# A Strassen-type scheme for the gates of a gated graph layer: seven f32 block products in place of eight

## The chip, the cores and the metric

The kernel runs on one core of a Trainium2 chip. The metric is device time in microseconds (us) of one execution.

## The reference, cut to what matters

128 graphs of 64 nodes with 256 features pass through four graph layers, each with a residual and a layer norm. Layer 3 is the large one: five rounds of message passing, each with a GRU cell whose gates are products with 256 x 768 weights.

```python
A = (adj != 0).astype(x.dtype)
h = x
for l in range(5):
    m = jnp.einsum('bnd,de->bne', h, weight[l])
    agg = jnp.einsum('bij,bid->bjd', A, m)
    gi = agg @ w_ih.T + b_ih            # r, z and n parts, 256 columns each
    gh = h @ w_hh.T + b_hh
    r = sigmoid(i_r + h_r);  z = sigmoid(i_z + h_z)
    n = tanh(i_n + r * h_n)
    h = (1.0 - z) * n + z * h
```

## The kernel before

It works on 16 chunks of 8 graphs, that is 512 nodes. Layer 0 is done first for all; then two chunks at a time go through layer 3 (`back`), while the middle layers 1 and 2 of the next two chunks (`mid`) run beside them. The weights `weight[l]` and `w_ih` are folded into one matrix `V` per round. Features lie on partitions in two halves `j` (outputs) and `k` (inputs), and nodes along the 512 columns of a bank of PSUM, the memory that takes TensorE's products (other tiles lie in SBUF). One round of one chunk:

```python
for j in range(2):
    pr, pz, pn, pi = (pg.tile([128, NP * 128], F32, tag="pg", name=f"p{s}") for s in ("r", "z", "n", "i"))
    for p, q, last in ((pn, 4 + j, True), (pr, j, False), (pz, 2 + j, False)):
        for k in range(2):
            nc.tensor.matmul(p, WHH[:, k, q * 128 : (q + 1) * 128], hT[:, k, :], start=k == 0, stop=last and k == 1)
    for p, q, first in ((pr, j, False), (pi, 4 + j, True), (pz, 2 + j, False)):
        for k in range(2):
            nc.tensor.matmul(p, V[:, l, k, q * 128 : (q + 1) * 128], agg[:, k, :], start=first and k == 0, stop=k == 1)
    # ... r: sigmoid (ScalarE); r = (pn + bhh) * r; r = pi + r (VectorE); n: tanh; z: sigmoid (ScalarE)
    nc.vector.tensor_sub(d, hT[:, j, :], n)
    nc.vector.tensor_mul(d, d, z)
    nc.vector.tensor_add(hn[:, j, :], d, n)
    if j == 0:
        yield
# ... then: transpose hn (TensorE), copy (ScalarE), gather the messages with A (TensorE), copy to agg
```

Each `yield` is a turn: the parts of the program take turns in being emitted, and a scheduler then fixes the order of instructions on each engine.

## Time and profile before

| | before |
|---|---|
| time | 2622.2 us, median of 3 (2618.42 to 2630.47) |
| TensorE busy | 2465.1 us, 94% |
| VectorE, ScalarE, GpSimd busy | 1064.3, 708.2, 113.6 us |
| gate products of layer 3 (3840 records of 429 ns) | 1647 us |
| TensorE's waits after 480 us | 45.2 us |

Names in the profile: PE is TensorE, PEld its weight loads, DVE VectorE, ACT ScalarE, POOL GpSimd; a record is one matmul instruction of the trace, two for each f32 product; PEclk is the clock that TensorE was granted, as a share of full speed. A row of 40 digits gives 40 equal slices of the run, in tenths. In a group's row stand line, engine, operation, output and inputs, shapes and count, then busy time, the mean of one in ns, and the engine's idle time just before with what ended it. A row in order of time starts with the start and the length in us; `x4` means four merged.

### The profile page before, as it was taken

What the parts mean: (1) busy time and instruction counts of PE and PEld (TensorE: products, weight loads), DVE (VectorE), ACT (ScalarE), POOL (GpSimd) and SP (SyncE); (2) the same over time, 40 slices, a digit from 0 to 9 for tenths busy, and PEclk for the clock granted to TensorE, in tenths of its full rate; (3) what the DMA queues carried; (4) which work ended last, traced back from release to release, by engine and by line L of the source; (5) the groups of instructions that cost most, each with busy time, mean ns of one, the idle gap of its engine ahead of it and who ended that gap; (6) DMA issues with size and microseconds to landing.
All of it is one profiled execution on the core that took longest, in us unless ns stands there. A gap on an engine that the chain in (4) does not pass through costs nothing.

```text
span 2617.6 us, 24051 instructions
## 1 busy us (share of the span) xinstructions
PE 2465.1 (94%) x9408; PEld 1442.0 (55%) x9408; DVE 1064.3 (41%) x2394; ACT 708.2 (27%) x1219; POOL 113.6 (4%) x108
## 2 busy tenths in 40 slices
PE   3999976999999999999999999999999999999998
PEld 2878865555455555555555545554555455544443
DVE  1342336444344444344434443544344434433234
ACT  1434330222222222222222222222223222222221
POOL 1100002000000000000000000000000000000000
PEclk9999997999999999999999999999999999999999
DMA  5222112000000000000000000000000000000000
GB/s 161 69 83 73 65 38 92 1 5 1 1 33 5 1 0 33 4 1 1 32 1 5 1 32 1 1 1 16 17 1 0 9 9 1 1 8 9 0 1 16
DMA packets 55281, 53.85 MB, mean 21 GB/s; under 512 B 24224, under 2 KB 48512, under 8 KB 55168
## 3 DMA queue, kind: packets, MB, share of 16 engines
q1 hardware_dynamic: 51616, 43.74, 5.3%
q0 software_dynamic: 1504, 5.51, 0.6%
q10 hardware_dynamic: 2048, 3.06, 0.4%
q8 instruction: 74, 1.21, 0.2%
q14 instruction: 39, 0.32, 0.0%
HBM read 35.52 MB, written 16.78 MB: 20 GB/s over the span
## 4 chain that ended last, share of the span: by engine, by line
PE 79%; DVE 12%; ACT 3%; DMA 2%; POOL 2%; issue 2%; SPq 1%; POOLq 0%; DVEq 0%; ACTq 0%
PE pz L529 10%; PE pr L524 10%; PE pz L524 10%; PE pr L529 10%; PE pi L529 10%; PE pa L415 8%; PE pn L524 5%; PE ps L280 5%; PE ph L265 4%; PE pT L552 2%; DVE d L542 2%; DVE hn L543 2%; DVE xt L108 2%; DVE st L101 2%; ACT zg L539 2%
## 5 line engine op out<-in xcount | busy, mean ns | idle before, releaser
L534 DVE SCALAR_TENSOR_TENSOR r<-pn,bhh,r 128x512 f32<-128x512 f32 x160 | 120.0, 750 | 897.0 <-ACT r L533 897.0
L533 ACT ACTIVATE r<-pr,brz 128x512 f32<-128x512 f32 x160 | 109.9, 687 | 969.8 <-PE pr L529 969.8
L529 PE MATMUL pr<-agg,V 128*128 128x512 f32 x640 | 300.7, 592 | 0.0
L529 PE MATMUL pz<-agg,V 128*128 128x512 f32 x640 | 300.7, 592 | 0.0
L529 PE MATMUL pi<-agg,V 128*128 128x512 f32 x640 | 300.7, 592 | 0.0
L524 PE MATMUL pr<-hn,WHH 128*128 128x512 f32 x512 | 243.2, 592 | 0.0
L524 PE MATMUL pn<-hn,WHH 128*128 128x512 f32 x512 | 240.7, 592 | 0.0
L524 PE MATMUL pz<-hn,WHH 128*128 128x512 f32 x512 | 240.6, 592 | 0.0
L529 PEld LDWEIGHTS pi<-agg,V 128*128 128x128 f32 x640 | 121.6, 190 | 153.1 <-issue 153.1
L529 PEld LDWEIGHTS pz<-agg,V 128*128 128x128 f32 x640 | 121.6, 190 | 153.1 <-issue 153.1
L529 PEld LDWEIGHTS pr<-agg,V 128*128 128x128 f32 x640 | 121.6, 190 | 153.1 <-issue 153.1
L537 ACT ACTIVATE n<-r,bih 128x512 f32<-128x512 f32 x160 | 115.4, 722 | 304.1 <-DVE r L535 297.0
L524 PEld LDWEIGHTS pz<-hn,WHH 128*128 128x128 f32 x512 | 96.7, 190 | 119.1 <-issue 117.4
L106 POOL TENSOR_TENSOR rs<-ve,mhalf 128x4 f32<-128x4 f32 x64 | 67.9, 1061 | 2002.1 <-DVE ve L104 2002.1
L552 PEld LDWEIGHTS pT<-ident,hn 128*128 128x128 f32 x640 | 74.5, 141 | 144.5 <-issue 143.6
L552 PE MATMUL pT<-ident,hn 128*128 128x128 f32 x640 | 98.7, 277 | 45.3 <-DVE hn L543 45.2
L524 PEld LDWEIGHTS pr<-hn,WHH 128*128 128x128 f32 x512 | 91.8, 191 | 88.5 <-issue 84.4
L524 PEld LDWEIGHTS pn<-hn,WHH 128*128 128x128 f32 x512 | 92.3, 190 | 85.8 <-issue 85.1
L541 DVE TENSOR_TENSOR d<-hn,n 128x512 f32<-128x512 f32 x128 | 88.6, 692 | 108.6 <-ACT n L537 108.6
L280 PE MATMUL ps<-W,hg 128*100 128x256 f32 (+3 forms) x576 | 131.1, 379 | 0.0
L415 PE MATMUL pa<-A,h 128*128 128x128 f32 x1024 | 127.8, 278 | 0.0
L415 PEld LDWEIGHTS pa<-A,h 128*128 128x128 f32 x1024 | 122.4, 191 | 0.0
(112 smaller groups left out, 2791.2 us busy)
## 6 DMA issues: line engine op xcount, KB each, us to landing
xt<-in_x_dram SPq DMA_DIRECT2D x16, 512.0 KB
x<-xt SPq DMA_DIRECT2D x16, 512.0 KB
xt<-x SPq DMA_DIRECT2D x16, 512.0 KB
out_dram<-xt SPq DMA_DIRECT2D x16, 512.0 KB
xg<-in_x_dram SPq DMA_DIRECT2D x32, 100.0 KB
W<-in_w_dram POOLq DMA_DIRECT2D x5, 512.0 KB, 9.1
W<-in_w_dram ACTq DMA_DIRECT2D x5, 512.0 KB
a<-in_adj_dram SPq DMA_DIRECT2D x16, 128.0 KB
```

The costliest lines, as they stand in the source:

```text
L101: nc.vector.bn_stats(st[:, p, :], y[:, p, :])
L106: nc.gpsimd.tensor_tensor(rs, ve, mhalf[:, :NP], ALU.pow)
L265: nc.tensor.matmul(p, W1[:, g, k, e * 128 : (e + 1) * 128], ag0[:, k, o : o + w], start=k == 0, stop=k == 1)
L280: nc.tensor.matmul(p[:r, h, :], hg[:, e, TOFF[t] - o : TOFF[t] - o + r], W2[:, g, e, :], start=e == 0, stop=e == 3,)
L415: nc.tensor.matmul(p[:, q * 128 : (q + 1) * 128], src[:, q, k * 128 : (k + 1) * 128], m[:, q, :], start=True, stop=True)
L524: nc.tensor.matmul(p, WHH[:, k, q * 128 : (q + 1) * 128], hT[:, k, :], start=k == 0, stop=last and k == 1)
L529: nc.tensor.matmul(p, V[:, l, k, q * 128 : (q + 1) * 128], agg[:, k, :], start=first and k == 0, stop=k == 1)
L533: nc.scalar.activation(r, pr, AF.Sigmoid, bias=brz[:, j : j + 1])
L534: nc.vector.scalar_tensor_tensor(r, pn, bhh[:, 4 + j : 5 + j], r, op0=ALU.add, op1=ALU.mult)
L537: nc.scalar.activation(n, r, AF.Tanh, bias=bih[:, 4 + j : 5 + j])
L541: nc.vector.tensor_sub(d, hT[:, j, :], n)
L552: nc.tensor.transpose(p[:, q * 128 : (q + 1) * 128], hT[:, k, q * 128 : (q + 1) * 128], ident)
```

## The change

A 2 x 2 block product takes eight block products. A scheme of the Strassen type takes seven, on sums of blocks, and adds the results up. Here the blocks are the halves of the inputs, of the outputs and of the nodes (H = 256 columns). The weight sums are made once. The sums of states and messages (`sums`, eight subtractions a round) are made on GpSimd; the results are added by VectorE out of PSUM, and partly by letting a product accumulate into a bank that has been read. The subtraction h - n moves from VectorE to GpSimd too. Buffers are cut to make room. The core of the diff, with cuts:

```diff
-    pg = ctx.enter_context(tc.tile_pool(name="pg", bufs=4, space=PSUM))
-    pt = ctx.enter_context(tc.tile_pool(name="pt", bufs=4, space=PSUM))
+    pg = ctx.enter_context(tc.tile_pool(name="pg", bufs=5, space=PSUM))
+    pt = ctx.enter_context(tc.tile_pool(name="pt", bufs=3, space=PSUM))
 ... (most tiles of the middle layers: one buffer in place of two)
+    def sums(a, name):
+        t = work.tile([128, 4, H], F32, tag="T" + name, name="T" + name, bufs=2)
+        nc.gpsimd.tensor_sub(t[:, 0, :], a[:, 0, H:], a[:, 0, :H])
+        nc.gpsimd.tensor_sub(t[:, 1, :], a[:, 1, H:], t[:, 0, :])
+        nc.gpsimd.tensor_sub(t[:, 3, :], a[:, 1, :H], t[:, 1, :])
+        nc.gpsimd.tensor_sub(t[:, 2, :], a[:, 1, H:], a[:, 0, H:])
+        return t
+    def two_gates(C, sides, name):
 ... (a, b, c, d: four PSUM banks; u2, u3: SBUF tiles)
+        products(a, 1, sides)
+        products(b, 6, sides)
+        nc.scalar.copy(u2, a)
+        nc.vector.tensor_add(u2, b, u2)
+        products(c, 7, sides)
+        nc.vector.tensor_add(u3, c, u2)
+        products(d, 5, sides)
+        nc.vector.tensor_add(C[:, :, 1, H:], d, u3)
+        products(a, 2, sides)
+        products(c, 4, sides)
+        nc.vector.tensor_add(C[:, :, 1, :H], c, u2)
+        products(d, 3, sides)
+        nc.vector.tensor_add(C[:, :, 0, H:], d, u2)
+        return a
 ... (in back, for each round; the old loop over j is gone)
+            p = two_gates(RZ, [[(WHH, q, hT, th), (V[l], q, agg, ta)] for q in (0, 1)], "rz")
 ... (sigmoids)
+            yield
+            p = two_gates(NI, [[(V[l], 2, agg, ta)], [(WHH, 2, hT, th)]], "n")
 ... (n = (h + bhh) * r + i, in three pieces, on VectorE)
+            for j in (1, 0):
+                nc.scalar.activation(n[:, j, :], n[:, j, :], AF.Tanh, bias=bih[:, 4 + j : 5 + j])
+                nc.gpsimd.tensor_sub(d[:, j, :], hT[:, j, :], n[:, j, :])
+                nc.vector.tensor_mul(d[:, j, :], d[:, j, :], RZ[:, 1, j, :])
+                nc.vector.tensor_add(hn[:, j, :], d[:, j, :], n[:, j, :])
 ...
-        interleave(b, a, *nxt)
+        interleave(b, a, both(*nxt))
```

More of the change, by code (lines that the diff above doesn't have):

```diff
@@ L25 @@
 CB = 8
+H = CB * N // 2
 NCH = B // CB
@@ L357, in load @@
     def load(c):
-        a64 = work.tile([128, NP, N], F32, name="a64", bufs=4)
+        a64 = work.tile([128, NP, N], F32, name="a64", bufs=2)
         nc.sync.dma_start(a64, av[c])
-        xt = work.tile([128, NP, D], F32, name="xt", bufs=6)
+        xt = work.tile([128, NP, D], F32, name="xt", bufs=5)
         nc.sync.dma_start(xt, x1[c])
@@ L371, in gnn_stack @@
     L2W = const(l2wT.rearrange("(k p) e -> p k e", p=128), [128, 2, D], "L2W")
-    WHH = const(whhT.rearrange("(k p) e -> p k e", p=128), [128, 2, 3 * D], "WHH", nc.gpsimd)
     bih = const(bihT, [128, 6], "bih")
@@ L382, in gnn_stack, with factors @@
         nc.vector.tensor_scalar(cI[:, k, :], ident, cw[:, k : k + 1], None, op0=ALU.mult)
-    V = wp.tile([128, L, 2, 3 * D], F32, name="V")
+    V = [wp.tile([128, 3, 7, 128], F32, name=f"V{l}") for l in range(L)]
+    WHH = wp.tile([128, 3, 7, 128], F32, name="WHH")
+    def factors(w, w21):
+        nc.vector.tensor_add(w[:, 4, :], w21, w[:, 3, :])
+        nc.gpsimd.tensor_sub(w[:, 6, :], w[:, 0, :], w21)
+        nc.vector.tensor_sub(w[:, 5, :], w[:, 4, :], w[:, 0, :])
+        nc.vector.tensor_sub(w[:, 2, :], w[:, 1, :], w[:, 5, :])
@@ L387, in fold @@
     def fold():
-        ih, wl = [], []
+        st = work.tile([128, 4, 2, D], F32, tag="RZ", name="ih", bufs=2)
+        whh = work.tile([128, 2, 3 * D], F32, tag="NI", name="whh", bufs=2)
         for q in range(3):
-            t = work.tile([128, 2, D], F32, tag="ew", name=f"ih{q}", bufs=12)
-            nc.gpsimd.dma_start(t, wihT[:, q * D : (q + 1) * D].rearrange("(k p) e -> p k e", p=128))
-            ih.append(t)
+            nc.gpsimd.dma_start(st[:, q], wihT[:, q * D : (q + 1) * D].rearrange("(k p) e -> p k e", p=128))
@@ L393, in fold @@
+        nc.gpsimd.dma_start(whh, whhT.rearrange("(k p) e -> p k e", p=128))
+        wl = work.tile([128, 4, 2, D], F32, tag="RZ", name="wl", bufs=2)
+        wls = [wl[:, l] for l in range(4)] + [st[:, 3]]
         for l in range(L):
-            t = work.tile([128, 2, D], F32, tag="ew", name=f"wl{l}", bufs=12)
-            nc.gpsimd.dma_start(t, wlT[l].rearrange("(k p) e -> p k e", p=128))
-            wl.append(t)
+            nc.gpsimd.dma_start(wls[l], wlT[l].rearrange("(k p) e -> p k e", p=128))
@@ L397, in fold @@
         yield
+        for q in range(3):
+            o = q * D
+            nc.scalar.copy(WHH[:, q, 0:2, :], whh[:, :, o : o + 128])
+            nc.scalar.copy(WHH[:, q, 3, :], whh[:, 1, o + 128 : o + D])
+            factors(WHH[:, q], whh[:, 0, o + 128 : o + D])
+            yield
         for l in range(L):
-            for j in range(2):
-                for q in range(3):
-                    p = psum("pf")
+            for q in range(3):
+                p = psum("pf").rearrange("p (j e) -> p j e", j=2)
+                for j in range(2):
@@ L402, in fold @@
                     for k in range(2):
                         nc.tensor.matmul(
-                            p[:, :D], wl[l][:, k, j * 128 : (j + 1) * 128], ih[q][:, k, :], start=k == 0, stop=k == 1
+                            p[:, j, :], wls[l][:, k, j * 128 : (j + 1) * 128], st[:, q, k, :], start=k == 0, stop=k == 1
                         )
-                    nc.vector.tensor_copy(V[:, l, j, q * D : (q + 1) * D], p[:, :D])
-                yield
+                w = V[l][:, q]
+                nc.scalar.copy(w[:, 0:2, :], p[:, :, 0:128])
@@ new lines, in fold @@
+                nc.scalar.copy(w[:, 3, :], p[:, 1, 128:256])
+                w21 = work.tile([128, 128], F32, name="w21", bufs=2)
+                nc.scalar.copy(w21, p[:, 0, 128:256])
+                factors(w, w21)
+                yield
+    def sums(a, name):
[5 more added lines that the diff above has]
+        return t
@@ new lines, in products @@
+    def products(bank, i, sides):
+        first = i in (1, 5, 6, 7)
+        n = len(sides[0])
+        for g, side in enumerate(sides):
+            for m, (w, q, a, t) in enumerate(side):
+                rhs = {1: a[:, 0, :H], 2: a[:, 1, :H], 3: a[:, 1, H:], 4: t[:, 3, :], 5: t[:, 0, :], 6: t[:, 1, :], 7: t[:, 2, :]}[i]
+                nc.tensor.matmul(
+                    bank[:, g, :], w[:, q, i - 1, :], rhs, start=first and g == 0 and m == 0, stop=m == n - 1,
+                    skip_group_check=True,
+                )
@@ new lines, in two_gates @@
+    def two_gates(C, sides, name):
+        a, b, c, d = (
+            pg.tile([128, 2, H], F32, tag="pg", name=f"p{s}{name}") for s in "abcd"
+        )
+        u2 = work.tile([128, 2, H], F32, name="u2", bufs=2)
+        u3 = work.tile([128, 2, H], F32, name="u3", bufs=2)
+        products(a, 1, sides)
[12 more added lines that the diff above has]
+        return a
@@ L409, in gather @@
     def gather(src, m, name, tag="ag"):
-        a = work.tile([128, 2, NP * 128], F32, tag=tag, name=name, bufs=3 if tag == "agg" else 2)
+        a = work.tile([128, 2, NP * 128], F32, tag=tag, name=name, bufs=2 if tag == "agg" else 1)
         for k in range(2):
@@ L425, in mid @@
         a64, xt = loaded.pop(c)
-        Ab = work.tile([128, NP, 128], F32, name="Ab", bufs=2)
+        Ab = work.tile([128, NP, 128], F32, name="Ab", bufs=1)
         nc.vector.tensor_mul(
@@ L443, in mid @@
         dinv1 = inv_sqrt(rdeg, NP, 128, "d1")
-        A1 = work.tile([128, NP, 128], F32, name="A1", bufs=2)
+        A1 = work.tile([128, NP, 128], F32, name="A1", bufs=1)
         nc.vector.tensor_add(A1, Ab, ident[:, None, :].to_broadcast([128, NP, 128]))
@@ L448, in mid @@
         yield
-        AT1 = work.tile([128, NP, 128], F32, name="AT1", bufs=2)
+        AT1 = work.tile([128, NP, 128], F32, name="AT1", bufs=1)
         p = psum("pT1").rearrange("p (q n) -> p q n", q=NP)
@@ L455, in mid @@
         nc.vector.tensor_mul(AT1, p, dinv1[:, :, None].to_broadcast([128, NP, 128]))
-        poly = work.tile([128, NP, 128], F32, tag="poly", name="poly3", bufs=4)
+        poly = work.tile([128, NP, 128], F32, tag="poly", name="poly3", bufs=2)
         p = psum("pT2").rearrange("p (q n) -> p q n", q=NP)
@@ L469, in mid @@
                 nc.tensor.matmul(p[:, q, :], Ab[:, q, :], poly[:, q, :], start=True, stop=True)
-            poly = work.tile([128, NP, 128], F32, tag="poly", name=f"poly{k}", bufs=4)
+            poly = work.tile([128, NP, 128], F32, tag="poly", name=f"poly{k}", bufs=2)
             nc.vector.tensor_add(poly, p, cI[:, k, None, :].to_broadcast([128, NP, 128]))
@@ L496, in mid @@
                     )
-            v = work.tile([128, 2, D], F32, name="v", bufs=2)
+            v = work.tile([128, 2, D], F32, name="v", bufs=1)
             nc.scalar.activation(v, p, AF.Identity, bias=cb)
@@ L514, in back @@
         agg = gather(xt, A01, "agg", "agg")
+        th, ta = sums(hT, "h"), sums(agg, "a")
         yield
@@ L517, in back @@
             hn = work.tile([128, 2, NP * 128], F32, tag="hT", name="hn", bufs=4)
-            for j in range(2):
-                pr, pz, pn, pi = (
-                    pg.tile([128, NP * 128], F32, tag="pg", name=f"p{s}") for s in ("r", "z", "n", "i")
-                )
-                for p, q, last in ((pn, 4 + j, True), (pr, j, False), (pz, 2 + j, False)):
-                    for k in range(2):
-                        nc.tensor.matmul(
-                            p, WHH[:, k, q * 128 : (q + 1) * 128], hT[:, k, :], start=k == 0, stop=last and k == 1
-                        )
-                for p, q, first in ((pr, j, False), (pi, 4 + j, True), (pz, 2 + j, False)):
-                    for k in range(2):
-                        nc.tensor.matmul(
-                            p, V[:, l, k, q * 128 : (q + 1) * 128], agg[:, k, :], start=first and k == 0, stop=k == 1
-                        )
-                r = work.tile([128, NP * 128], F32, tag="ew", name="r", bufs=12)
-                nc.scalar.activation(r, pr, AF.Sigmoid, bias=brz[:, j : j + 1])
-                nc.vector.scalar_tensor_tensor(r, pn, bhh[:, 4 + j : 5 + j], r, op0=ALU.add, op1=ALU.mult)
-                nc.vector.tensor_add(r, pi, r)
-                n = work.tile([128, NP * 128], F32, tag="ew", name="n", bufs=12)
-                nc.scalar.activation(n, r, AF.Tanh, bias=bih[:, 4 + j : 5 + j])
-                z = work.tile([128, NP * 128], F32, tag="ew", name="zg", bufs=12)
-                nc.scalar.activation(z, pz, AF.Sigmoid, bias=brz[:, 2 + j : 3 + j])
-                d = work.tile([128, NP * 128], F32, tag="ew", name="d", bufs=12)
-                nc.vector.tensor_sub(d, hT[:, j, :], n)
-                nc.vector.tensor_mul(d, d, z)
-                nc.vector.tensor_add(hn[:, j, :], d, n)
-                if j == 0:
-                    yield
@@ new lines, in back @@
+            RZ = work.tile([128, 2, 2, NP * 128], F32, tag="RZ", name="RZ", bufs=2)
+            p = two_gates(RZ, [[(WHH, q, hT, th), (V[l], q, agg, ta)] for q in (0, 1)], "rz")
+            for q in range(2):
+                nc.scalar.activation(RZ[:, q, 0, :H], p[:, q, :], AF.Sigmoid, bias=brz[:, 2 * q : 2 * q + 1])
+            for q in range(2):
+                nc.scalar.activation(RZ[:, q, 1, :], RZ[:, q, 1, :], AF.Sigmoid, bias=brz[:, 2 * q + 1 : 2 * q + 2])
+                nc.scalar.activation(RZ[:, q, 0, H:], RZ[:, q, 0, H:], AF.Sigmoid, bias=brz[:, 2 * q : 2 * q + 1])
@@ new lines, in back @@
+            yield
+            NI = work.tile([128, 2, 2, NP * 128], F32, tag="NI", name="NI", bufs=2)
+            p = two_gates(NI, [[(V[l], 2, agg, ta)], [(WHH, 2, hT, th)]], "n")
+            n, d = NI[:, 1], RZ[:, 0]
+            for j, f, i, h in (
+                (0, slice(0, H), p[:, 0, :], p[:, 1, :]),
+                (1, slice(0, 2 * H), NI[:, 0, 1, :], n[:, 1, :]),
+                (0, slice(H, 2 * H), NI[:, 0, 0, H:], n[:, 0, H:]),
+            ):
+                nc.vector.scalar_tensor_tensor(
+                    n[:, j, f], h, bhh[:, 4 + j : 5 + j], RZ[:, 0, j, f], op0=ALU.add, op1=ALU.mult
+                )
+                nc.vector.tensor_add(n[:, j, f], i, n[:, j, f])
@@ L546, in back @@
+            for j in (1, 0):
[3 more added lines that the diff above has]
+                nc.vector.tensor_add(hn[:, j, :], d[:, j, :], n[:, j, :])
             hT = hn
             if l < L - 1:
-                h = work.tile([128, NP, D], F32, name="h", bufs=2)
+                th = sums(hT, "h")
+                h = work.tile([128, NP, D], F32, name="h", bufs=1)
@@ L564, in back @@
                 agg = gather(h, A01, "agg", "agg")
+                ta = sums(agg, "a")
             yield
@@ L567, in back, with both @@
         nc.sync.dma_start(ov[c], xt)
-    interleave(mid(0), mid(1), fold())
+    def both(*gens):
+        for g in gens:
+            yield from g
+    interleave(both(mid(0), mid(1)), fold())
     for u in range(0, NCH, 2):
```

## The prediction

> **What bounds the kernel now.** I read the page's engine totals and the slices first, then the groups of instructions, then the matmuls in order of time, last the list of waits.
>
> ```profile
> PE 2465.1 (94%) x9408; PEld 1442.0 (55%) x9408; DVE 1064.3 (41%) x2394; ACT 708.2 (27%) x1219; POOL 113.6 (4%) x108
> ...
> PE   3999976999999999999999999999999999999998
> ```
>
> TensorE is busy 94% of 2617.6 us. The slices show where the other 152 us lie: the first slice (inputs arriving) and slices 5 and 6, some 330 to 460 us, where layer 0 ends and layers 1 and 2 and the folding of weights start. From about 480 us to the end TensorE is full, so there its work is the time. Which work, the groups tell:
>
> ```profile
> L529 PE MATMUL pr<-agg,V 128*128 128x512 f32 x640 | 300.7, 592 | 0.0
> ...
> L524 PE MATMUL pn<-hn,WHH 128*128 128x512 f32 x512 | 240.7, 592 | 0.0
> ...
> L534 DVE SCALAR_TENSOR_TENSOR r<-pn,bhh,r 128x512 f32<-128x512 f32 x160 | 120.0, 750 | 897.0 <-ACT r L533 897.0
> ```
>
> The gate products of layer 3 are 3 x 640 records at line 529 and 3 x (512 + 128) at line 524: 3840 records, two for each of the 1920 f32 products. Their busy time double counts the pipeline's tail (592 ns each), so the pace must come from the matmuls in order of time:
>
> ```profile
> 1501.59 1.88 PE L524 MATMUL pr<-hn,WHH 128*128 128x512 f32 x4
> 1503.30 1.88 PE L524 MATMUL pz<-hn,WHH 128*128 128x512 f32 x4
> ```
>
> Four records start every 1.716 us: 429 ns a record. 3840 x 0.429 = **1647 us**, 63% of the span. A 256-column record is there too:
>
> ```profile
> 431.07 7.07 PE L478 MATMUL pd<-L1W,ag 128*128 128x256 f32 x32
> 437.98 2.75 PE L403 MATMUL pf<-ih,wl 128*128 128x256 f32 x12
> ```
>
> 32 records in 437.98 - 431.07 = 6.91 us: 216 ns each, with new weights for every record, so the weight load stays hidden. In layer 3 TensorE waits for one thing only:
>
> ```profile
> PE pT L552 <- DVE hn L543: 45.2, 71, 2.0
> ```
>
> 45.2 us in 71 waits: the transposes of a chunk's new state wait for the last vector operation of its gates. The other chunk of the pair covers the rest.
>
> **What the Trainium skill says.** "TensorE: Matmul & The Clock Gate", section "Back-to-back issue gap", gives N / 2.4 + 2.5 ns for a warm matmul. With two streams of the columns per f32 record that is 429.2 and 215.8 ns: the trace agrees (429, 216), so halving the columns costs TensorE nothing. "GPSIMD Engine Reference", section 3.1, gives 4497 ns for a two-input f32 add of 2048 elements; scaled by elements, an estimate from that page, 256 elements take some 0.6 us and 512 some 1.2 us with start-up. The trace has no such operation (its GpSimd powers of 4 elements took 1061 ns). "SBUF — State Buffer", section "Who interferes with whom": a VectorE instruction with two SBUF inputs and a GpSimd instruction that reads SBUF exclude each other for a whole instruction. No row here shows it, GpSimd being nearly idle. "PSUM — Partial Sum Buffer", section "PSUM bank collisions raise a hardware error": two engines must not be on one bank at once, so a product that accumulates into a bank that VectorE still reads has to wait.
>
> **Part by part.** A gate of one chunk and layer needs, on each side (state, messages), 4 products of 512 columns, that is 8 of 256. After: 7 of 256.
>
> Removed from and added to TensorE: before, 24 products x 2 records x 80 (16 chunks x 5 layers). After, (28 + 14) products x 2 records x 80 = 6720 records x 0.216 = 1452 us. Saving 1647 - 1452 = **195 us**, if the products run as densely as now. Folding of the weights keeps 120 records of 256.
>
> VectorE, per chunk and layer. Before: 2 x (750 + 4 x 692 ns) = 7.0 us. After: ten sums out of PSUM (u2, u3 and three stores, for two pairs of gates) at 692 ns = 6.9 us; reset-gate products of 256, 512, 256 columns, 0.48 + 0.75 + 0.48 (256 scaled between the 750 ns of 512 and 345 ns of 128 columns); three adds 0.43 + 0.69 + 0.43 (0.43 near the 406 ns of 256-column statistics); four operations of 692 ns at the end. Sum 12.9 us, or +5.9 us, x 80 = +472 us: VectorE goes from 1064 to some 1540 us, about 60% of the span.
>
> ScalarE: two copies of 586 ns and two more sigmoid starts per chunk and layer, some +1.5 us x 80 = +120 us: 830 us in all. Off the path in total.
>
> GpSimd: 8 subtractions of 256 and 2 of 512 elements per chunk and layer, 8 x 0.6 + 2 x 1.2 = 7.2 us x 80 = 580 us, up from 114: not a bound by total.
>
> So by totals TensorE remains the bound; its dense limit is 2617.6 - 195 = 2423 us even with today's idle time. What matters is the new waits. The instruction order of the changed kernel shows, in nearly every round of layers: products of r and z for chunk B, for chunk A, then n of B, n of A, then B's transposes, its gather, its next r and z with A's transposes set into them. Only one n phase, 14 products x 2 x 0.216 = 6.05 us, covers the tail of the other chunk's gates. Before it was a 10.3 us step (24 records x 0.429).
>
> What must be done under it: an n phase has five PSUM sums, 2 x (0.48 + 0.69 + 0.43) and so on: 3.5 + 3.3 + 2.8 = 9.5 us of VectorE by single durations, some 8.5 us when independent ones overlap their starts (the trace issues such 128x512 operations some 70 ns closer). Two n phases are 17 to 19 us of VectorE against 12.1 us of TensorE. In order: first chunk's last product ends at 6.05 us; until its new state stands VectorE still has to do the last store and products (3.1 us), the last multiply and add of two halves (2.8 us), and, set between them, the other chunk's first sums (2.1 us), with a tanh (0.72) and a GpSimd subtraction (1.2) in the chain: about 8 us of work and 0.5 to 1 us of bubble, so 14.5 against the 12.1 us: 1.5 to 3 us of wait at the transposes. Then A's transposes come only 4 to 7 us into the next r and z products, while A's subtractions queue on GpSimd behind the sums of the new messages (4 x 0.6 us): 0 to 2.5 us. The sums themselves hold the second product of r and z by 0 to 0.7 us. Where a layer norm lies in VectorE's queue between the evictions (it waits 1.2 us for GpSimd in today's trace) the n phase stretches by 2 us or more. I take 4.2 us for a round, 40 rounds: 170 us of waits, against 45 now. So **net = -195 + (170 - 45) = -70 us**.
>
> The start of layers 1 to 3: two chunks' middle layers go one after the other now, not side by side, but weight folding fills between them; +-10 us, counted as 0.
>
> **Rivals.** (1) The saving comes nearly whole. For it: the scheduler's order in the kernel before turned out well (45 us in 160 transposes), all engines stay under 65%, banks have slack (a bank is reused two products, 1.7 or 3.5 us, after the product VectorE must read). Against: the 6.05 us cover. Time about 2622 - 190 = 2435 us. (2) VectorE with GpSimd becomes the bound of the n phases: each exclusion on the shared port costs up to 0.7 or 1.2 us, and four to eight VectorE operations of a round's tail have two SBUF inputs. Waits of 6.5 to 8 us a round, 260 to 320 us in all: 2640 to 2700 us, same or slower. (3) The reduced buffers (single copies of the middle layers' tiles, 3 instead of 4 general PSUM banks) make the next chunks' middle work wait. It has two whole chunk times of slack, so I give it under 20 us; it would show as idle at the transposes or gathers of the middle layers.
>
> **Range and chances.** From the median of 2622.2: 2622 - 70 = 2552, and I say 2550 us. The size of the wait per round decides: 2 us gives some 2465, 7 us some 2665. So 2450 to 2665 for 8 in 10. Faster by over 2% means under 2570 us, that is under 4.6 us of wait per round, which my sum just meets; rival 1 adds weight: 0.6. Same 0.31, slower 0.09.
>
> **What would show each step.** Right: 6720 gate records at 216 ns; TensorE's busy share falls to about 90%, VectorE near 1500 us, GpSimd at 600 to 750; new waits of TensorE on VectorE at the transposes, near 100 us, and on VectorE and GpSimd at the products, near 50 us. Wrong: records above 216 ns (weight loads no longer hidden); GpSimd subtractions of 256 elements much over 0.6 us, or VectorE operations lengthened by the port, giving the slow end; idle under 80 us in layer 3, giving the fast end.

## More of the kernel before

The lines that carry the argument are in the prediction. One more is needed for comparison, the busy time of each engine in layer 3 (the stretch, its length, busy time and instructions of TensorE, weight loads, VectorE, ScalarE and GpSimd, then the granted TensorE clock):

```profile
480.00:2610.00 2130.00, 2082.47 (x7122) 1120.79 (x7120) 883.68 (x1765) 563.97 (x885) 55.15 (x51) 1.00 0.02 7
```

TensorE is busy in 2082 of 2130 us here, at full clock.

## The result

| | before | after |
|---|---|---|
| time, median | 2626.0 us (4 runs) | 2811.0 us (4 runs, 2802.1 to 2813.9) |
| ratio | | 1.070, 95% interval 1.066 to 1.074 |

A ratio is the mean time of one kernel's fast runs over that of the other's in the same rounds, so it is not quite the ratio of the medians. The changed kernel is correct and **slower by 7%**. The profiled runs spanned 2617.6 and 2809.4 us, which makes 191.8 us to explain.

First the engine totals of the changed kernel, the slices of TensorE and of its clock, and layer 3 alone:

```profile
PE 2370.0 (84%) x12288; PEld 2045.3 (73%) x12288; DVE 1577.8 (56%) x3218; ACT 830.9 (30%) x1590; POOL 804.3 (29%) x926
...
PE   3999958888798888988798888887888798879886
...
PEclk9999979999899999999999999999999999999998
```

```profile
480.00:2800.00 2320.00, 1984.61 (x9995) 1720.11 (x9993) 1396.35 (x2583) 674.51 (x1206) 740.52 (x855) 0.95 0.02 7
```

TensorE is no longer full: its slices of layer 3 went from 9 to mostly 7, 8 or 9. VectorE is at 56% and GpSimd at 29%, so neither has become a bound by its total. The products run as fast as they should, as the matmuls in order of time show:

```profile
1501.99 0.59 PE L445 MATMUL parz<-hn,WHH 128*128 128x256 f32 x2
1502.42 0.59 PE L445 MATMUL parz<-agg,V 128*128 128x256 f32 x2
```

Two records in 0.43 us are 216 ns each. The list of TensorE's waits after 485 us (total, times, longest) tells where the time went:

```profile
PE pT L614 <- DVE hn L606: 244.0, 62, 9.7
PE pcn L445 <- DVE u L462: 37.7, 25, 2.4
PE pbrz L445 <- POOL Ta L433: 29.8, 26, 1.4
PE pdn L445 <- DVE NI L464: 17.3, 15, 1.5
```

The wait for a chunk's new state, 45.2 us before, is now 244.0 us. All waits in this stretch sum to 334.8 us. One such wait, on all engines in order of time:

```profile
1546.98 0.59 PE L445 MATMUL pan<-hn,WHH 128*128 128x256 f32 x2
1547.35 1.33 ACT L603 ACTIVATE NI<-NI,bih 128x512 f32<-128x512 f32 x2 [4.08 <-DVE NI L601]
...
1548.14 2.49 POOL L604 TENSOR_TENSOR RZ<-hn,NI 128x512 f32<-128x512 f32 x2 [5.49 <-ACT NI L603]
1549.44 2.33 DVE L605 TENSOR_TENSOR RZ<-RZ 128x512 f32<-128x512 f32 x2 [0.86 <-POOL RZ L604]
1551.70 1.28 DVE L606 TENSOR_TENSOR hn<-RZ,NI 128x512 f32<-128x512 f32 x2
```

TensorE's last product starts at 1546.98; the new state stands at 1552.98, and the transposes start at 1553.04 after 5.46 us idle. Of those, two GpSimd subtractions take 2.49 us, and two multiplications that wait for them take 2.33 us, where the two additions after them take 1.28 us. Over the whole run the groups say the same:

```profile
L604 POOL TENSOR_TENSOR RZ<-hn,NI 128x512 f32<-128x512 f32 x128 | 162.8, 1286 | 390.9 <-ACT NI L603 390.9
L605 DVE TENSOR_TENSOR RZ<-RZ 128x512 f32<-128x512 f32 x160 | 172.7, 1090 | 120.4 <-POOL RZ L604 120.4
```

The multiplication took 692 ns before and 1090 ns now, with the same shapes.

The third loss is the clock. Two stretches after a wait follow, first after the 5.46 us wait, then after a wait of 1.85 us at 1511.3 us:

```profile
1546.98:1553.04 6.06, 0.60 (x3) 0.19 (x2) 5.20 (x9) 1.33 (x2) 2.49 (x2) 0.78 0.00 0
1553.04:1557.84 4.80, 4.80 (x25) 4.52 (x25) 1.48 (x3) 1.76 (x3) 2.95 (x5) 0.57 0.02 5
...
1511.30:1516.40 5.10, 5.06 (x42) 4.80 (x43) 0.59 (x1) 2.83 (x5) 4.40 (x7) 1.00 0.00 0
```

After the long wait TensorE's granted clock is 0.57, and 25 instructions fill 4.80 us; after the short one it is 1.00, and 42 fill 5.06 us. The trace's clock records hold 39 spells at half clock between 485 us and TensorE's last product, 242 us in all, against 2 spells and 7 us before. All 22 waits of over 3.4 us in the changed kernel are followed by such a spell. The other 17 spells follow waits of 1.5 to 2.7 us, though most waits of that size have none; the two spells before follow waits of 2.02 us (749.0 to 752.4 us at a clock of 0.50).

**The sum.** In layer 3 TensorE is busy for 1984.6 us. With the products' saving (195 us, as in the prediction; the paces over all records at full clock, 429.3 and 215.9 ns, would give 198, so the split is good to some 3 us) and nothing else it would be 2082.5 - 195 = 1887.5 us, so the same work took 97.1 us longer. Waits rose from 45.2 to 334.8 us. Together: -195 + 97.1 + 289.6 = 191.7 us, against 191.8 measured. That the sum closes is bookkeeping, as busy time and waits fill the stretch; it shows only that the whole loss lies in layer 3. Of the 97 us the clock explains most, not all: TensorE was busy for 153 us within the spells, which loses 76 us at half clock. The other 20 us are not shown apart; an estimate from the number of waits (151 after 485 us, 72 before) is 0.2 to 0.3 us for each further wait, where one record's end no longer overlaps the next record.

### The profile page after: what moved, and what is told of

The parts are those of the page before. It is cut to its first block, busy times and chain, and to the rows that moved or that the text cites. A ratio compares the mean times of both kernels' runs of the same rounds, so it can differ in the third digit from the quotient of the medians.

```text
span 2809.4 us, 32059 instructions
## 1 busy us (share of the span) xinstructions
PE 2370.0 (84%) x12288; PEld 2045.3 (73%) x12288; DVE 1577.8 (56%) x3218; ACT 830.9 (30%) x1590; POOL 804.3 (29%) x926
## 3 DMA queue, kind: packets, MB, share of 16 engines
q10 hardware_dynamic: 2048, 3.06, 0.3%
## 4 chain that ended last, share of the span: by engine, by line
PE 57%; DVE 21%; POOL 8%; issue 7%; ACT 3%; DMA 2%; SPq 1%; DVEq 0%; POOLq 0%; ACTq 0%
PE pdrz L445 8%; PE parz L445 8%; PE pcrz L445 8%; PE pa L478 7%; PE ps L281 4%; POOL RZ L604 4%; PE pT L614 3%; PE ph L266 3%; DVE RZ L605 3%; DVE NI L598 3%; PE pbrz L445 2%; DVE hn L606 2%; DVE NI L601 2%; PE pdn L445 2%; PE pcn L445 2%
## 5 line engine op out<-in xcount | busy, mean ns | idle before, releaser
L614 PE MATMUL pT<-ident,hn 128*128 128x128 f32 x640 | 115.0, 338 | 244.0 <-DVE hn L606 244.0
L604 POOL TENSOR_TENSOR RZ<-hn,NI 128x512 f32<-128x512 f32 x128 | 162.8, 1286 | 390.9 <-ACT NI L603 390.9
L605 DVE TENSOR_TENSOR RZ<-RZ 128x512 f32<-128x512 f32 x160 | 172.7, 1090 | 120.4 <-POOL RZ L604 120.4
L445 PE MATMUL pcrz<-Th,WHH 128*128 128x256 f32 x640 | 193.2, 384 | 0.0
L445 PE MATMUL parz<-agg,V 128*128 128x256 f32 x640 | 192.3, 382 | 0.1
L445 PE MATMUL pcrz<-Ta,V 128*128 128x256 f32 x640 | 190.4, 379 | 0.0
L603 ACT ACTIVATE NI<-NI,bih 128x512 f32<-128x512 f32 x160 | 112.2, 720 | 184.4 <-DVE NI L601 183.6
L445 PE MATMUL parz<-hn,WHH 128*128 128x256 f32 x512 | 154.5, 384 | 0.0
L445 PEld LDWEIGHTS pcrz<-Th,WHH 128*128 128x128 f32 x640 | 121.7, 193 | 15.6
L445 PEld LDWEIGHTS pcrz<-Ta,V 128*128 128x128 f32 x640 | 120.3, 190 | 15.7
L445 PEld LDWEIGHTS parz<-agg,V 128*128 128x128 f32 x640 | 118.4, 190 | 15.2 <-ACT agg L481 0.3
```

The costliest lines, as they stand in the source:

```text
L445: nc.tensor.matmul(bank[:, g, :], w[:, q, i - 1, :], rhs, start=first and g == 0 and m == 0, stop=m == n - 1, skip_group_check=True,)
L603: nc.scalar.activation(n[:, j, :], n[:, j, :], AF.Tanh, bias=bih[:, 4 + j : 5 + j])
L604: nc.gpsimd.tensor_sub(d[:, j, :], hT[:, j, :], n[:, j, :])
L605: nc.vector.tensor_mul(d[:, j, :], d[:, j, :], RZ[:, 1, j, :])
L614: nc.tensor.transpose(p[:, q * 128 : (q + 1) * 128], hT[:, k, q * 128 : (q + 1) * 128], ident)
```

## The experiments

Two theories were set against each other. Theory A: in the order of emission, the tail of one chunk's gates has only the other chunk's n products as cover. Theory B: GpSimd, by its slow instruction in the chain and by the SBUF port that it shares with VectorE, makes the tail long. In the table, "waits" are all of TensorE's waits after 485 us, "half clock" is the time at half clock from there to TensorE's last product, and "excess" is TensorE's busy time in layer 3 over 1887.5 us (for e7 less some 36 us of added work, an estimate).

| kernel | time, us | ratio to before | waits | half clock | excess |
|---|---|---|---|---|---|
| before | 2619 to 2622 | 1 | 45 | 7 | |
| after | 2811.0 | 1.070 | 335 | 242 | 97 |
| e1: h - n on VectorE | 2687.6 | 1.026 | 207 | 219 | 98 |
| e3: h - n and sums on VectorE | 2647.3 | 1.010 | 189 | 168 | 76 |
| e4: new order | 2716.6 | 1.038 | 284 | 133 | 54 |
| e5: new order, h - n on VectorE | 2577.7 | 0.985 | 157 | 130 | 42 |
| e7: after, with filling work | 2798.6 | 1.067 | 293 | 177 | 92 |
| e8: e5 without stops between pairs | 2482.1 | 0.946 | 76 | 51 | 27 |
| e9: e8, h - n on GpSimd | 2626.2 | 1.001 | 205 | 86 | 42 |
| e10: e8, sums on VectorE | 2412.4 | 0.919 | 32 | 5 | 0 |
| e11: e10, h - n on GpSimd | 2581.7 | 0.986 | 171 | 50 | 31 |
| e12: e10, useless GpSimd work | 2553.5 | 0.975 | 150 | 23 | 24 |

All gave correct results; all intervals are within 0.4% of the ratio. The runs of before in the three sets had medians of 2619.5, 2621.6 and 2618.5 us.

One caution holds for all of them: the scheduler orders each kernel anew, so an operation moved to another engine moves the transposes too. In half of the chunk rounds of after they stand 10 or 17 products into the other chunk's next r and z products, in e1 13 or 19, in e3 20 or 19 (a product takes 0.43 us). Only e10 and e12 have the same order on TensorE throughout.

### e1: one subtraction back on VectorE

```diff
-                nc.gpsimd.tensor_sub(d[:, j, :], hT[:, j, :], n[:, j, :])
+                nc.vector.tensor_sub(d[:, j, :], hT[:, j, :], n[:, j, :])
```

> The changed kernel with one edit: the subtraction h - n at the end of the gates goes back from GpSimd to VectorE (the eight sums stay on GpSimd). Theory A (order: the gates' tail of one chunk has only the other chunk's n products, 6.05 us, as cover): the tail gets shorter by about two times 1.29 - 0.69 us and by the port waits of the multiplications (1.09 instead of 0.69 us), some 1.5 to 2 us a round, so the 244 us of waits at the transposes fall to some 150, half-clock time falls with them, 2811 becomes 2680 to 2730: still slower than before. Theory B (GpSimd in the chain and the shared port are the cause by themselves): waits at the transposes fall below 80 us and the time below 2600.

It took 2687.6 us, 123 us less, with waits on the new state of 146.9 us: what theory A expected of this edit; theory B's range (below 2600 us) was missed. Yet a move of one operation, with the later transposes that came with it, is worth 123 us, so theory B holds a part.

### e3: no GpSimd arithmetic in layer 3

Beside e1's edit, `nc.gpsimd` becomes `nc.vector` in the four lines of `sums`.

> The changed kernel with all new GpSimd arithmetic of the layers (the h - n subtraction and the eight sums) on VectorE: no GpSimd instruction can hold the shared port in layer 3. VectorE gets some 2 x 0.69 + 8 x 0.43 = 4.8 us more per chunk and layer, about +380 us busy (to 1850 us with the port waits gone). Theory A: the order is kept, so long waits stay, 2680 to 2800, multiplications back at 692 ns. Theory B (port): below 2600. A third view, that VectorE's load is what binds: slower than the changed kernel, over 2811.

It took 2647.3 us, a little below the range of theory A and above that of theory B, so both missed. VectorE's load, 1766 us, did not bind. The multiplication is back at its old length:

```profile
L605 DVE TENSOR_TENSOR RZ<-RZ 128x512 f32<-128x512 f32 x160 | 106.6, 684 | 0.0
```

So GpSimd as a whole, with the transposes that it moves, costs 164 us in the old order, and even without it the kernel stays 1% slower than before.

### e4 and e5: another order of emission

```diff
-            yield
             NI = work.tile([128, 2, 2, NP * 128], F32, tag="NI", name="NI", bufs=2)
 ...
         next(a)
+        next(b)
         next(a)
-        interleave(b, a, both(*nxt))
+        m = both(*nxt)
+        interleave(b, m, a, m)
```

A chunk's r, z and n products of a round are now one turn, so the other chunk's r and z products (12.1 us) follow its n products. e5 has e1's edit as well.

> The changed kernel with another order of emission only: a chunk's r, z and n products of one layer are emitted together (the pause between them removed), both chunks of a pair are set up before their first layer, and the next chunks' middle layers get two turns a round. Every operation and engine is unchanged. The tail of one chunk's gates is then covered by the other chunk's r and z products (12.1 us) in place of its n products (6.05 us). Theory A: waits of TensorE on the new state fall from 244 us to under 80, half-clock time after 485 us from 250 to under 80, time 2480 to 2580. Theory B: the GpSimd chain and port waits remain, time within 2% of 2811.

> Both: the new order of e4_order and the h - n subtraction on VectorE as in e1_sub_dve. Theory A: a little better than e4_order, as the tail is shorter than the 12.1 us cover in nearly all rounds: 2450 to 2540, waits on the new state under 40 us. Theory B: as e1_sub_dve.

Both missed theory A's range, and theory B's (within 2% of 2811 us; as e1) too: e4 took 2716.6 us and e5 2577.7 us. In e4 the transposes still wait, 194.2 us in 80 times (72 of 1.3 to 1.8 us, 8 of about 8.4 us at the ends of pairs). The multiplication has become longer still:

```profile
L604 DVE TENSOR_TENSOR RZ<-RZ 128x512 f32<-128x512 f32 x160 | 193.0, 1209 | 116.2 <-POOL RZ L603 116.2
```

The scheduler had also put the transposes earlier with the subtraction on GpSimd (in the static order, 17 products after the chunk's last n product in e4, 19 in e5), so the longer tail met a shorter cover. Those two products, 0.86 us in 72 of the waits, are up to some 60 of the 139 us between e4 and e5 (an estimate). In e5 the waits on the new state are 59.5 us, and all of them are 8 waits of about 7.5 us: the ends of the eight pairs of chunks, where nothing is left to cover the last round. The same ends hold waits of 46.5 and 27.7 us on the middle layers' norm (the expectation of e8 has 57.6, which counts two waits before 485 us).

### e7: filling the waits

```diff
+            if c % 2:
+                pw = psum("pw")
+                for j in (1, 0):
+                    for q in range(NP):
+                        nc.tensor.transpose(pw[:, q * 128 : (q + 1) * 128], n[:, j, q * 128 : (q + 1) * 128], ident)
```

> The changed kernel with eight extra 128-column transposes of the tanh outputs n per layer of each odd chunk, into a PSUM tile nobody reads: they run while TensorE waits for that chunk's new state, and shorten no chain. If the waits cost a second time through TensorE's clock, the half-clock time after 485 us falls from 250 us to under 120 and the granted clock rises from 0.947 to over 0.97, busy time of the real work falls by 40 to 90 us, and the time falls by 20 to 80 us below 2811 although 40 x 8 x 0.11 = 35 us of work were added. If the clock is only a side effect that costs nothing, the time stays or grows by up to 35 us.

It took 2798.6 us, 12 us less, with 177 us at half clock and a clock of 0.958. This is a miss: half clock fell less than expected, the time fell by less than 20 us, and the excess only from 97 to 92 us. The filling work stands in TensorE's order, waits itself (53.6 us for the tanh), and then leaves the transposes another 164.9 us to wait. Work put into the waits is no cure. That the clock's loss comes from the waits rests on the spells read above and on the table, where half clock and excess fall together down to 5 and 0 us in e10; no run changed the clock alone.

### e8, e9, e10: no stops between pairs

```diff
+    def setup(c):
+        while c not in state:
+            next(m)
 ... (first transposes, gather and sums of chunk c, as at the head of back before)
             p = two_gates(NI, [[(V[l], 2, agg, ta)], [(WHH, 2, hT, th)]], "n")
+            if l == L - 1 and c + 2 < NCH:
+                setup(c + 2)
 ...
-    for u in range(0, NCH, 2): ...
+    def middles():
+        loaded[2] = load(2)
+        for c in range(2, NCH):
+            if c + 1 < NCH:
+                loaded[c + 1] = load(c + 1)
+            yield from mid(c)
+    def chain(first):
+        for c in range(first, NCH, 2):
+            yield from back(c)
+    setup(0); setup(1)
+    a, b = chain(0), chain(1)
+    next(a)
+    interleave(b, m, a, m)
```

e8 is e5 with two endless chains of chunks in place of pairs. e9 has h - n on GpSimd again, e10 has the sums on VectorE too.

> e5_order_sub_dve with the stops between pairs of chunks taken away: the next chunk of each chain is set up (transposes, first gather, sums) inside the last layer of the chunk before it, after its products, and the middle layers of coming chunks run as one stream, loaded one chunk ahead. If what is left in e5 are the eight pair ends (waits of 59.5 on the new state, 57.6 and 27.7 us on the middle layers' norm, and 143 us at half clock), these vanish: waits in layer 3 under 40 us, half clock under 50 us, 2400 to 2470 us, some 6 to 8% under the kernel before. If the seven products themselves are not worth their 195 us, it stays near 2560.

> e8_roll_setup with the h - n subtraction back on GpSimd, as in the changed kernel. In the instruction order the transposes then stand one 0.43 us product after the other chunk's fourth r and z product, not three. By e4 against e5 (139 us apart, waits of 194 against 59.5 us) the GpSimd chain of 2 x 1.27 us plus port waits should cost again some 1.5 to 2 us at each of 80 layers: 120 to 160 us above e8. If e4's loss came only from pair ends, under 30 us above e8.

> e8_roll_setup with the eight sums on VectorE too, nothing of layer 3's arithmetic on GpSimd. VectorE gets some 8 x 0.43 us x 80 = 270 us more work, near 1770 us of 2430. If port waits and GpSimd's 0.73 us sums still cost something in e8: 10 to 40 us faster. If VectorE's load begins to bind: 10 to 60 us slower than e8.

e8 took 2482.1 us, 5.4% under the kernel before but 12 us above its range: 76 us of waits and 50 us at half clock remained. e9 took 2626.2 us, 144 us more for one subtraction, inside its range. e10 took **2412.4 us, 8.1% under the kernel before**, 70 us less than e8 and better than its range. Its totals and its layer 3:

```profile
PE 2275.4 (94%) x12288; PEld 1985.8 (82%) x12288; DVE 1761.4 (73%) x4018; ACT 816.1 (34%) x1590; POOL 118.6 (5%) x126
...
PE   3999994899999999999999999999999999999997
```

```profile
480.00:2409.00 1929.00, 1887.95 (x9994) 1659.12 (x9992) 1584.31 (x3399) 659.61 (x1206) 55.92 (x56) 1.00 0.03 9
```

TensorE's busy time of layer 3 is 1887.95 us, where 2082.5 - 195 = 1887.5 us was worked out: the seven products give their whole saving once next to nothing waits. The kernel before could not win as much by order alone, as all its waits in layer 3 are 45 us; its own rearrangement was not run.

After, e3, e9 and e10 make a table of two by two. The old order costs 2811 us with GpSimd arithmetic and 2647 without; the new one 2626 and 2412. Either step gains 164 or 185 us alone, and both together 399.

### e11 and e12: what about GpSimd costs

```diff
-                nc.vector.tensor_sub(d[:, j, :], hT[:, j, :], n[:, j, :])
+                nc.gpsimd.tensor_sub(d[:, j, :], hT[:, j, :], n[:, j, :])
```

e12 leaves e10's line and puts useless work on GpSimd ahead of it. TensorE's instruction order is then the same as e10's.

```diff
+                scr = work.tile([128, NP * 128], F32, name="scr", bufs=1)
+                nc.gpsimd.tensor_sub(scr, hT[:, j, :], n[:, j, :])
                 nc.vector.tensor_sub(d[:, j, :], hT[:, j, :], n[:, j, :])
```

> e10_roll_no_pool with the h - n subtraction alone on GpSimd (the sums stay on VectorE). The instruction order then puts the transposes one product later or earlier in the other chunk's second a product than in e10. If the subtraction in the chain is what costs in e9 (144 us over e8), it costs 110 to 150 us here too, without any sums on GpSimd: 2520 to 2560. If e9 was slow because subtraction and sums queue on one GpSimd, under 50 us: below 2460.

> e10_roll_no_pool with a second, useless h - n subtraction on GpSimd at the same place, into a tile nobody reads; VectorE still does the real one, so no chain goes through GpSimd, and TensorE's instruction order is the same as e10's. Only the shared port is tested. If the exclusion on the port is most of what GpSimd costs: VectorE's two-input operations at the end of the gates grow by up to 0.6 us each and the time rises by 60 to 140 us. If GpSimd's longer instruction in the chain is most of it: VectorE's operations grow, but the time rises by less than 40 us.

e11 took 2581.7 us, 169 us over e10, more than the 110 to 150 expected; the sums are not needed for the loss. e12 took 2553.5 us, 141 us over e10 (a hair above the range given for the port), although no result of GpSimd is used. VectorE's real subtraction and GpSimd's own, 1.27 us where least disturbed (e4), now hold each other up. First e10's line, then e12's:

```profile
L612 DVE TENSOR_TENSOR RZ<-hn,NI 128x512 f32<-128x512 f32 x128 | 87.2, 687 | 15.9 <-ACT NI L611 15.2
...
L614 DVE TENSOR_TENSOR RZ<-hn,NI 128x512 f32<-128x512 f32 x128 | 161.0, 1264 | 17.3 <-ACT NI L611 16.9
L615 DVE TENSOR_TENSOR RZ<-RZ 128x512 f32<-128x512 f32 x160 | 139.6, 880 | 0.1
...
L613 POOL TENSOR_TENSOR scr<-hn,NI 128x512 f32<-128x512 f32 x128 | 205.7, 1607 | 882.3 <-ACT NI L611 877.8
```

This is the exclusion that the Trainium skill states in "SBUF — State Buffer", section "Who interferes with whom". VectorE waits for GpSimd's results no longer in e12 than in e10 (34.0 against 36.5 us after 485 us, nearly all for the layer norm), but its busy time rises by 137 us (1761.4 to 1898.6 us). So the exclusion by itself can cost 141 us. It doesn't follow that it is 141 of e11's 169 us: there GpSimd's subtraction holds up another operation, the multiplication (1124 ns, 683 in e10; 160 times, 71 us), VectorE waits 98.9 us for the longer subtraction, and most transposes stand two products earlier than in e10. How the 169 us divide between these three is open.

## Why the prediction was wrong

It said 2550 us with a range to 2665 and 0.6 for faster; the kernel took 2811 us. Step by step:

- **The saving on TensorE was right.** 6720 records ran at 216 ns, and e10 shows the full 195 us (1887.95 against 1887.5 us). That the weight load stays hidden was right too.
- **The engines' totals were about right.** VectorE was predicted at some 1540 us and measured at 1577.8, ScalarE 830 and 830.9. GpSimd was to reach 580 + 114 = 694 us and reached 804: 256 elements took 0.73 us, not 0.6, and up to 0.90 beside VectorE. None of them became a bound by its total.
- **The wait per round was mis-sized.** The step was right in kind: the n phase's 6.05 us do not cover the other chunk's tail. Of "I take 4.2 us for a round, 40 rounds: 170 us" the runs made 334.8 / 40 = 8.4 us. The port was named in rival 2 as costing "up to 0.7 or 1.2 us", but the working for the 4.2 us took 692 ns for the multiplications, which took 1090. Most of the miss is at the transposes: it expected near 100 us there and near 50 us at the products, and the runs gave 244.0 and 90.8 us. The sums themselves held the products as predicted (29.8 / 40 = 0.7 us a round); what the norm's operations in VectorE's queue cost was not measured apart. With nothing on GpSimd (e3) the old order waits 189 us, 4.7 us a round: the predicted size is near that of a kernel without the port.
- **Rival 2 was the nearest** (6.5 to 8 us a round, 2640 to 2700 us) and still ended too low, by the next point.
- **A term was missing: the clock.** The sum counted a wait only as long as it lasts. The Trainium skill says in "TensorE: Matmul & The Clock Gate", section "HAM oscillation — how this bites in real kernels", that idle gaps above some 3.4 us bring TensorE back to half clock; the prediction used that page for the pace alone. Here 39 spells at half clock followed waits of 1.5 to 9.7 us; they cost 76 us of the 97 us by which the same work took longer. Without those 97 us, the measured waits give 2617.6 - 195 + 289.6 = 2712 us, already outside the range: the mis-sized wait is enough by itself for the miss.
- **Rival 3 was rightly left small.** The cut buffers are in e10 as well, which waits for 32 us in all.
- **Rival 1 was not the outcome, but it was the potential.** It named 2435 us; e10 reaches 2412 us with the same products after the order and the engine were changed.

## What to carry to other kernels

When an operation count falls on the engine that bounds, ask what the shorter work had been covering: here the dependent tail grew while its cover shrank from 10.3 to 6.05 us. Off-loading to an idle GpSimd is not free beside VectorE operations with two SBUF inputs; one subtraction a half round cost 123 to 169 us of time in four pairs of kernels, the moved transposes included, and 141 us in e12, where TensorE's order stayed. Count a TensorE wait of several us once for its length and once more for the slower clock after it (here 335 us of waits and 76 us).

## What the Trainium skill lacked or had wrong

- "SBUF — State Buffer": the exclusion on the shared port is there, and e12 agrees, but of its size only two ratios, 6.8 for VectorE and 1.5 for GpSimd, without the operations. Here two simultaneous 128x512 subtractions took 1264 ns (VectorE, 687 alone) and 1607 ns (GpSimd, 1268 in e4), and the kernel lost 141 us.
- "GPSIMD Engine Reference": one size of add, 4497 ns for 2048 elements, that is 2.2 ns an element. The runs give 726 ns for 256 and 1268 for 512 elements: 2.1 ns an element, and a start-up of some 0.18 us (726 - 256 x 2.1, an estimate); the page names the steps of the start but no total.
- "TensorE: Matmul & The Clock Gate": its formula for the pace agrees with the trace (216 and 429 ns). Its rule of 3.4 us for the clock holds one way: all 22 longer waits of the changed kernel brought half clock. It is too mild the other way: 17 of 39 spells there followed waits of 1.5 to 2.7 us, and both spells of the kernel before waits of 2.02 us. What decides among the shorter waits is open.
- No page on these engines says that an instruction order fixed before the run can meet a longer tail than it was made for. In e4, 72 waits of 1.3 to 1.8 us (127 us) stand before transposes that were mostly placed 17 products after the tail began.
